# Graph layer with sorted edges: gate, hot logits and own rows move from the bank of the constants to a bank of their own, and the sorting's scratch shrinks to one bank

## Chip, cores, metric

The kernel runs on one core of one Trainium2 chip, as one launch. The metric is the device time of that core in microseconds (us). Engines are called as in the profile: PE (matrix products and transposes; PEld are its weight loads), DVE (vector), ACT (activation), POOL (here it only issues gathers) and SP (issues most DMAs).

## What is computed

A graph layer over 12,500 nodes of 128 features and 412,500 edges that are sorted by destination (`dst`), followed by a residual and a layer norm:

```
theta = x[dst] - x[src]
w     = sigmoid(relu(theta @ W1 + b1) @ W2 + b2)
agg   = segment_sum(w * theta, dst)
indeg = segment_sum(ones, dst)
out   = layernorm(x + agg + indeg * (x @ W4 + b4))
```

## The kernel before

**Stages.** First a table `z` in DRAM is built with, for each node, `x @ W1` beside `x` (`table_chunk`, L748 on). Then the edges are worked through in 276 parts. The first 18 (`PLAIN`) have 1,024 edges each and every source row is gathered for them (`early_part`). Parts 18 to 275 have 1,532 edges each (`part`): 1,024 of these are gathered from `z` by source node, the other 512 have sources in small ranges of nodes, the "hot" ones, and their rows are made from tables in SBUF by products with one-hot tiles. Two parts make one block (104 output rows). `part(s)` is called with `h == 0` for even and `h == 1` for odd `s`; a pair of parts is one round of the main stage.

**One part, engine by engine.** The main loop runs under a manual schedule: PE, DVE and ACT carry out their instructions in the order in which the code issues them, so the order of the lines in `part` is the order of each engine's queue.

- PE: L1076/L1077 (hidden layer of the hot edges of part s+1, into bank `pz`), L885 (`spread_y`: destination rows for the edges of part s+2, into one of two `y` banks), L1090 (`hot_rows`: four hot logits columns of part s+1), L1093 (hot rows turned into `pz`), L1049 (hot products for a later part, into `pd`), then the sums into `pa`: in an even part `add_block` (L1130: `sh`, eight `wxh`, four `wx` products), in an odd part `begin_block` (L1141, L1142, L807, four L1130).
- DVE: L988 (`weigh`: half of the previous part's gathered rows times their gate), L943 (destination minus source rows; this frees the `y` bank that L885 writes next), L948 (relu times `w2_b`), L918 (`one_hot_w`, reads `iota_f`; before L954 in even parts, after it in odd ones), L954 (sum to the logits `lg`); then in an even part L1112 (`one_hot_h`, reads `iota_f`), in an odd part L1195 and at its end `normalize` (L1223 to L1248). Between them stand the steps of the sorting.
- ACT: L1082 (relu of the hot hidden layer, `hr`, which L1090 reads), one-hot tiles L864/L865, in odd parts L1184, L812, L1124, L1125, then L1099 (sigmoid of the hot logits), four L1102 (weighted hot rows), in odd parts L1203/L1205 (`own`: this block's own rows), L960 (`open_gate`: sigmoid of `lg` into `gate`), L966, L970, four L995, then L1033/L1035 (one-hot tiles for L1049), L1063.
- POOL: eight indirect gathers of a part (L398), for part s+3 in `part(s)`. The first of the eight waits for the newest PE instruction at that place (`paced`), the sums of the part before.

**The sorting.** `place` is a generator that splits the edges of the next 64 parts (a set) into hot and gathered ones on DVE, with some PE and ACT. The sets begin at parts 18, 82, 146, 210 and 274; the first is placed during the early parts, the others during the main stage. Each `yield` names a kind of step: "k" for the many short ones (32 rounds of L580, L581, L583 and L576, that work in SBUF alone), "s", "p", "m" and "c" for longer ones. `spend` issues steps at the end of each part against a credit of 2.5 per part, at a price of 0.85 for a "k", 2.5 for an "m" and 3.5 for an "s" or "p". Some steps use a scratch tile in PSUM: the two sums of L534 to L547, the four scans (L636 to L657, an "s" each), the nine moves (L670 to L676, an "m" each) and the transposes L609 and L701. In the main stage the scratch is `px`, a tile of two PSUM banks (1,024 fp32).

**PSUM.** There are eight banks: `fix`, two of `y`, `pz`, `pd`, `pa` and the two of `px`. `fix` holds five things (L290 to L297): `iota_f` and `w2_b`, constants that DVE reads in L918, L1112 and L948; `own_f`, which ACT writes in L1205 and DVE reads and writes in L1223 and reads in L1229; `lgh`, which PE writes in L1090 and ACT reads in L1099; `gate`, which ACT writes in L960 and DVE reads in L988. The language layer that the kernel is written in puts in all semaphores. It orders two accesses from different engines to one PSUM tile also where they touch different columns.

Of the kernel before, what the change touches and what calls it, by code (L numbers as in the profile page):

```python
# [9 lines left out]
F32 = mybir.dt.float32  # L10
BF16 = mybir.dt.bfloat16
F16 = mybir.dt.float16
I32 = mybir.dt.int32
U16 = mybir.dt.uint16
AF = mybir.ActivationFunctionType
OP = mybir.AluOpType
# [4 lines left out]
P = 128  # L21
D = 128
K = 8
# [3 lines left out]
SUB = 2  # L27
WB = 104
# [4 lines left out]
G = 4  # L33
# [16 lines left out]
HX = HB + 1  # L50
RG = 4
HK = HR * HS
HQ = HK // P
# [13 lines left out]
WL = HL + 1  # L67
# [3 lines left out]
HKL = HR * HE  # L71
# [4 lines left out]
MOVES = 9  # L76
# [6 lines left out]
def gnn_resnorm(  # L83
# [37 lines left out]
    nc = tc.nc  # L121
# [3 lines left out]
    NS = PLAIN - (E1 - E) // CE  # L125
# [12 lines left out]
    while n0 < N:  # L138
        t = max(1, (N - n0) // P)
# [115 lines left out]
    w2_c = const.tile([P, 1], F32, name="w2_c")  # L255
# [25 lines left out]
    for i, t in enumerate(terms):  # L281
        at = slice(i * HALF // 2, i * HALF // 2 + 1)
# [7 lines left out]
    cps = ctx.enter_context(tc.tile_pool(name="ps_c", bufs=1, space=bass.MemoryType.PSUM))  # L290
    fix = cps.tile([P, 512], F32, name="fix")
    iota_f = fix[:, :WB].rearrange("p (o m) -> p o m", o=1)
    own_f = fix[:, WB:WB + D]
    w2_b = fix[:, WB + D:WB + 2 * D]
    lgh = fix[:, 512 - 2 * K - SUB * HQ:512 - 2 * K].rearrange("p (i q) -> p i q", q=HQ)
    gate = fix[:, 512 - 2 * K:].rearrange("p (i k) -> p i k", k=K)
    w2_f = w2_r.rearrange("p (o m) -> p o m", o=1)  # L297

    oh_all = const.tile([P, NO * RW], F32, name="oh")
# [57 lines left out]
    for t in wxe_buf:  # L357
        nc.vector.memset(t[:, :, D + 1:], 1.0)
    late_at = 2 * G * P + 2 * K * AW
    assert late_at + 2 * NS <= HX * HK and WB + 2 * D + 2 * K + SUB * HQ <= 512  # L360
    hot_src = const.tile([P, NU, RG * HB * HS], F16, name="hot_src")
    hots = {}

# [7 lines left out]
    def filled(t, s):  # L371

        if s < NF:
            return t
        return t.rearrange("p (h j) d -> p h j d", h=2)[:, :, :JT, :]
# [121 lines left out]
    def place(i, scratch, es, ed, bb, dp):  # L497
# [8 lines left out]
        v = nc.vector  # L506
# [17 lines left out]
        for r in rows:  # L524
            v.scalar_tensor_tensor(b[r, 3:4], c[r, 2:3], float(NOT - WB + 1), c[r, 18:19],
                                   op0=OP.add, op1=OP.add)
        yield "s"

        t = ep.tile([P, WL], F32, name="et")
# [7 lines left out]
        C = -(-HL // 2)  # L537
        for j in range(2):
            at = slice(j * C, min(j * C + C, HL))
            m = at.stop - at.start  # L540
            step = scratch()[:, :m]
            v.tensor_sub(step, ed[:, at.start + 1:at.stop + 1], ed[:, at])
            q = ep.tile([P, P * G], F32, name="eq")[:, :m]
# [30 lines left out]
        for r in range(HR):  # L574
            if r:
                v.scalar_tensor_tensor(left, left, float((HR - r + 1) * AREA), left,  # L576
                                       op0=OP.is_lt, op1=OP.mult)
# [20 lines left out]
                        op0=OP.logical_shift_right, op1=OP.bitwise_and)  # L598
# [12 lines left out]
        for q in range(HQ):  # L611
            for h in range(LISTS):
                a, e = max(h * HKL - q * P, 0), min((h + 1) * HKL - q * P, P)
# [12 lines left out]
        w = ep.tile([P, WL], I32, name="ed")  # L626
        NC = 4
        C = -(-WL // NC)
        assert 3 * C <= WL - HKL // 2 and 2 * HKL <= WL - HKL // 2 and 2 * C < 2 * P * G
        for j in range(NC):  # L630
            at = slice(j * C, min(j * C + C, WL))
            m = at.stop - at.start
            pw = scratch()[:, :2 * P * G]
            odd, count = pw[:, :m + 1], pw[:, C + 1:C + 1 + m]
            keep, out_, mark = (free[:, k * C:k * C + m] for k in range(3))
            v.tensor_scalar(keep, t[:, at], float(NOT * BIG), None, op0=OP.is_ge)  # L636
            v.scalar_tensor_tensor(mark, t[:, at], float(BIG), keep, op0=OP.is_ge, op1=OP.add)
            v.tensor_scalar(mark, mark, -1.0, 1.0, op0=OP.mult, op1=OP.add)
            if j:
                v.tensor_copy(odd[:, :1], c[:, 5:6])  # L640
            else:
                v.memset(odd[:, :1], 0.0)
            v.tensor_tensor_scan(odd[:, 1:], mark, keep, c[:, 5:6] if j else 0.0,
                                 op0=OP.mult, op1=OP.add)
            v.tensor_copy(c[:, 5:6], odd[:, m:])
            v.scalar_tensor_tensor(mark, mark, 0.0, odd[:, :m], op0=OP.is_equal, op1=OP.mult,
                                   accum_out=c[:, 6 + j:7 + j])
            v.tensor_add(keep, keep, mark)
            v.scalar_tensor_tensor(w[:, at], t[:, at], float((2 * NOT - 1) * BIG), keep,
                                   op0=OP.min, op1=OP.mult)  # L650
            v.tensor_scalar(out_, keep, -1.0, 1.0, op0=OP.mult, op1=OP.add)
            v.tensor_tensor_scan(count, out_, most.to_broadcast([P, m]),
                                 c[:, 4:5] if j else 0.0, op0=OP.add, op1=OP.min)
            v.tensor_copy(c[:, 4:5], count[:, m - 1:])
            move = out_.bitcast(I32)
            v.tensor_mul(move, count, keep)
            v.scalar_tensor_tensor(w[:, at], move, 31 - MOVES, w[:, at], op0=OP.logical_shift_left,  # L657
                                   op1=OP.bitwise_or)
            yield "s" if j < NC - 1 else "m"
# [8 lines left out]
        assert SW + HKL < 1 << MOVES and BIG << 8 == 1 << (31 - MOVES) and MOVES % 2 and WL <= 2 * P * G  # L668
        for r, m in enumerate([1 << r for r in range(MOVES)]):
            u = ep.tile([P, WL], I32, name="ew" if r % 2 else "et")  # L670
            bit = scratch().bitcast(I32)[:, :WL]
            v.tensor_scalar(bit, w, MOVES - r, 31, op0=OP.logical_shift_left, op1=OP.arith_shift_right)
            v.scalar_tensor_tensor(u, bit, -1, w, op0=OP.bitwise_xor, op1=OP.bitwise_and)
            v.copy_predicated(u[:, :WL - m].bitcast(F32), bit[:, m:], w[:, m:].bitcast(F32))
            yield "m" if r < MOVES - 1 else "z"
            w = u  # L676
        to = ep.tile([P, WL], I32, name="ed")[:, :BL]
        v.tensor_scalar(to, w[:, :BL], BIG.bit_length() - 1, 2 * NOT - 1,
                        op0=OP.logical_shift_right, op1=OP.bitwise_and)
# [31 lines left out]
    with tc.manual_schedule(engines={SP}), tc.tile_pool(name="work", bufs=2) as wp, tc.tile_pool(  # L711
# [25 lines left out]
        def wide():  # L737

            return ps_l.tile([P, 2 * P * G], F32, name="px")
# [183 lines left out]
        def logits(s):  # L923
# [31 lines left out]
            if s % SUB:  # L955
                one_hot_w(s)

        def open_gate(s):

            nc.scalar.activation(filled(gate[:, s % 2].rearrange("p (k e) -> p k e", e=1), s),  # L960
                                 filled(parts[s]["lg"], s), AF.Sigmoid, bias=b2_c)

        def gate_sums(s):
# [8 lines left out]
        def weigh(s):  # L972

            zs = rows_of(s)
            if s < PLAIN:
                wx = wx_of(s)
                for k in range(K):
                    nc.scalar.activation(wx[:, k, :D], zs[:, k, :] if s < NH else zs[:, k, D:],
                                         AF.Copy, scale=wx[:, k, D:D + 1])
                return  # L980
            w = gate[:, s % 2].rearrange("p (k e) -> p k e", e=1)
            wx = wx_of(s)[:, :, :D]
            if s < NF:
                xs = zs[:, :KV, D:]
                w, wx = w[:, :KV], wx[:, :KV]
            else:
                xs, w, wx = filled(zs[:, :, D:], s), filled(w, s), filled(wx, s)
            nc.vector.tensor_tensor(wx, xs, w.to_broadcast(list(xs.shape)), op=OP.mult)  # L988
# [84 lines left out]
        def hot_turned(t):  # L1073

            xT = xT_all[:, (t - PLAIN) % HX, :]
            nc.tensor.matmul(pz, wneg, xT, start=True, stop=False)  # L1076
            nc.tensor.matmul(pz, y_of(t), blocks[t // SUB]["oh"][:, BP:], start=False, stop=True)  # L1077
# [6 lines left out]
        def hot_rows(t):  # L1084

            xT = xT_all[:, (t - PLAIN) % HX, :]
            hr = parts[t]["hr"]
            for q in range(HQ):
                at = slice(q * P, (q + 1) * P)
                nc.tensor.matmul(lgh[:, t % SUB, q:q + 1], hr[:, at], w2_c, start=True, stop=True)  # L1090
            for q in range(HQ):
                at = slice(q * P, (q + 1) * P)
                newest[0] = nc.tensor.transpose(pz[:, at], xT[:, at], ident)  # L1093

        def hot_weights(t):

            b, h = divmod(t, SUB)
            wx = wxh_buf[b % len(wxh_buf)][:, h * HQ:(h + 1) * HQ, :]
            nc.scalar.activation(wx[:, :, D:D + 1], lgh[:, h].rearrange("p (q e) -> p q e", e=1),  # L1099
                                 AF.Sigmoid, bias=b2_c)  # L1100
            for q in range(HQ):
                nc.scalar.activation(wx[:, q, :D], pz[:, q * P:(q + 1) * P], AF.Copy,  # L1102
                                     scale=wx[:, q, D:D + 1])
# [93 lines left out]
        def own(b):  # L1197

            d = blocks[b]
            a = d["a"]  # L1200
            plain = b * SUB < PLAIN
            sw = wp.tile([P, 2], F32, name="sw")
            nc.scalar.activation(sw[:WB], a[:WB, D:AW], AF.Copy, bias=1.0)  # L1203
            d["own"] = d["xw"][:WB] if plain else own_f[:WB]
            nc.scalar.activation(d["own"], d["xw"][:WB], AF.Copy, scale=sw[:WB, 0:1])  # L1205
            d["deg"] = a[:WB, D + 1:AW] if plain else sw[:WB, 1:]

# [127 lines left out]
        def early_part(s):  # L1335
# [19 lines left out]
            while opened:  # L1355
                hot_out(*opened.pop(0))
            if s == PLAIN - 1:
                hot_turned(PLAIN)
                hot_relu(PLAIN)
            if h and b:  # L1360
# [84 lines left out]
        for t in (wx_buf[EW], *wxh_buf):  # L1445
            nc.vector.memset(t[:, :, D + 1:], 1.0)
        add_up(PLAIN - 1)
        px = wide()
        where[0] = lambda: px

        def spread_ahead(s):

# [273 lines left out]
```

## Time and profile before

| | |
|---|---|
| median of three runs | 3246.63 us (3229.67 to 3252.84) |
| profiled execution: its own time | 3245.33 us |
| profiled execution: span from first to last instruction | 3243.3 us |
| busy in the span | PE 2793.9, DVE 2413.1, ACT 2456.1, POOL 2163.7 us |
| mean granted PE clock | 0.880 |

In a row of a group the columns are line, engine, operation, tiles written and read, count, busy time and mean duration of one, then the engine's idle time before these and what ended it. In a row of the waits they are the engine and line that waited, what it waited for, us in total, times and the longest. A row of the timeline has start and duration in us, engine, line, operation and, in brackets, the idle time before it.

### The profile page before, as it was taken

To read this page: it belongs to the slowest core of one execution; us is meant where nothing else is said; L and a number is where in the kernel's file an instruction comes from. 1 tells how busy PE (TensorE), PEld (TensorE's weight loads), DVE (VectorE), ACT (ScalarE), POOL (GpSimd) and SP (SyncE) were. 2 spreads that over 40 slices of the span, in tenths; PEclk is the share of its full clock that TensorE was granted. 3 is DMA by queue.
4 is the path that set the end of the run, shared out by engine and by line. 5 is a ranking of instruction groups with operands and counts; after the bars stand their busy time and mean duration, and the time that the engine had idled before them with its cause. 6 is when DMAs were issued, how large, how long until landed. Compare 5 with 4: busy or idle time off the path is not lost.

```text
span 3243.3 us, 53854 instructions
## 1 busy us (share of the span) xinstructions
PE 2793.9 (86%) x16422; PEld 2346.8 (72%) x16422; DVE 2413.1 (74%) x4015; ACT 2456.1 (76%) x6397; POOL 2163.7 (67%) x2213
## 2 busy tenths in 40 slices
PE   6868889898888889888898988989898988888896
PEld 5667777777767777777776777767776776777675
DVE  7997677777767877777667787777657778877654
ACT  5447777787788787777887777878887778778875
POOL 3675676776666676766676677766676777766662
PEclk7768888888899898898998889989988899988988
DMA  7564444444444444444454444444444444444441
GB/s 246 159 175 115 116 125 125 118 129 114 126 132 125 120 130 121 123 125 123 131 149 112 124 123 127 129 118 127 122 133 112 126 122 132 129 111 124 127 123 49
DMA packets 239303, 413.24 MB, mean 127 GB/s; under 512 B 63423, under 2 KB 147226, under 8 KB 237470
## 3 DMA queue, kind: packets, MB, share of 16 engines
q0 software_dynamic: 105280, 286.93, 31.8%
q1 hardware_dynamic: 131756, 116.40, 13.9%
q10 hardware_dynamic: 1970, 6.40, 0.6%
q8 instruction: 132, 2.16, 0.3%
q14 instruction: 165, 1.35, 0.1%
HBM read 388.57 MB, written 20.94 MB: 126 GB/s over the span
## 4 chain that ended last, share of the span: by engine, by line


## 5 line engine op out<-in xcount | busy, mean ns | idle before, releaser
L398 POOL DMA_INDIRECT zbuf<-z,src_i x2060 | 2013.1, 977 | 931.3 <-issue 371.9
L1049 PE MATMUL pd<-of,tabs 128*128 128x128 f32 (+2 forms) x4240 | 666.8, 325 | 0.0
L1049 PEld LDWEIGHTS pd<-of,tabs 128*128 128x128 f32 x4240 | 649.7, 242 | 0.0
L1130 PE MATMUL pa<-wx,ow 128*104 128x260 f32 (+1 forms) x2284 | 542.9, 384 | 1.8 <-DVE wx L988 1.8
L1090 PE MATMUL fix<-w_c,hr 128*128 128x1 f32 x2064 | 308.1, 270 | 226.9 <-DVE ow L918 197.7
L885 PEld LDWEIGHTS y<-y,oh 128*128 128x128 f32 (+1 forms) x2108 | 274.7, 196 | 283.4 <-DVE zbuf L943 215.3
L1090 PEld LDWEIGHTS fix<-w_c,hr 128*128 128x128 f32 x2064 | 294.6, 220 | 253.1 <-ACT sh L1125 103.0
L1130 PEld LDWEIGHTS pa<-wx,ow 128*104 128x104 f32 x2284 | 377.7, 180 | 82.9 <-issue 2.9
L1112 DVE TENSOR_TENSOR owh<-fix,hrel 128x832 f32<-128x832 f32 x129 | 132.2, 1025 | 410.5 <-ACT fix L960 398.8
L885 PE MATMUL y<-y,oh 128*128 128x128 f32 (+1 forms) x2108 | 299.1, 286 | 118.6 <-DVE zbuf L943 108.1
L1082 ACT ACTIVATE hr<-pz 128x512 f32<-128x512 f32 x258 | 154.0, 597 | 286.9 <-PE pz L1077 286.8
L1102 ACT ACTIVATE wxh<-pz,wxh 128x128 f32<-128x128 f32 x1032 | 295.2, 369 | 88.7 <-PE pz L1093 86.1
L1033 ACT ACTIVATE of<-hot_src,nodes 128x512 f32<-128x512 f16 (+2 forms) x530 | 343.9, 696 | 3.5 <-PE pd L1049 2.4
L948 DVE SCALAR_TENSOR_TENSOR zbuf<-zbuf,fix 128x1024 f32<-128x1024 f32 x273 | 331.6, 1215 | 13.4 <-ACT wxh L1099 4.1
L954 DVE TENSOR_REDUCE lg<-zbuf 128x8 f32<-128x1024 f32 x273 | 329.9, 1209 | 5.0
L995 ACT ACTIVATE wx<-zbuf,wx 128x128 f32<-128x128 f32 x1028 | 328.7, 390 | 0.0
L943 DVE TENSOR_TENSOR zbuf<-y,zbuf 128x1024 f32<-128x1024 f32 x258 | 313.6, 1216 | 0.0
L1035 ACT ACTIVATE of<-of 128x1024 f32<-128x1024 f32 (+1 forms) x265 | 274.1, 1035 | 8.4
L1076 PE MATMUL pz<-xT,wni 128*128 128x512 f32 x516 | 266.2, 598 | 1.1 <-ACT wxh L1102 1.1
L1077 PE MATMUL pz<-oh,y 128*128 128x512 f32 x516 | 266.3, 598 | 0.2 <-ACT oh L865 0.2
L1130 PE MATMUL pa<-wxh,owh 128*104 128x130 f32 x2064 | 260.0, 280 | 0.0
L1130 PEld LDWEIGHTS pa<-wxh,owh 128*104 128x104 f32 x2064 | 248.0, 175 | 0.0
(302 smaller groups left out, 4103.0 us busy)
## 6 DMA issues: line engine op xcount, KB each, us to landing
to_all<-off_d SPq DMA_DIRECT2D x258, 128.0 KB
zbuf<-z,src_i POOLq DMA_INDIRECT x2060
hot_src<-hot_s SPq DMA_DIRECT2D x228, 128.0 KB
z<-zbuf SPq DMA_DIRECT2D x10, 1024.0 KB
y<-z SPq DMA_DIRECT2D x270, 28.0 KB
xw<-in_x_dram SPq DMA_DIRECT2D x138, 52.0 KB
out_dram<-o SPq DMA_DIRECT2D x138, 52.0 KB
wx<-in_x_dram ACTq DMA_DIRECT2D x12, 512.0 KB
```

What stands on the lines that cost most here:

```text
L398: ins = nc.gpsimd.indirect_dma_start(out=rows_of(s)[:, k, :], out_offset=None, in_=z if s >= NH else x, in_offset=IndirectOffsetOnAxis(ap= ...
L885: nc.tensor.matmul(y[:, j, :], d["oh"][:, (k0 + j) * P:(k0 + j + 1) * P], y_of(s), start=True, stop=True)
L943: nc.vector.tensor_sub(half, yy.to_broadcast([P, 2, n, D]), half)
L948: nc.vector.scalar_tensor_tensor(h[:, at, :], h[:, at, :], 0.0, w2.to_broadcast([P, n, D]), op0=OP.max, op1=OP.mult)
L954: nc.vector.tensor_reduce(lg[:, at, 0], h[:, at, :], AX.X, OP.add)
L995: nc.scalar.activation(wx[:, k, :D], rows_of(s)[:, k, D:], AF.Copy, scale=wx[:, k, D:D + 1])
L1033: nc.scalar.activation(of[:, t, :], hot_src[:, i % NU, :w], AF.Abs, bias=nodes[:, t:t + 1])
L1035: nc.scalar.activation(of, of, AF.Relu, scale=-1.0, bias=1.0)
L1049: newest[0] = nc.tensor.matmul(to[:, q], tabs[:, g * RG + q, t, :], of[:, t, q], start=t == 0, stop=t == HT - 1)
L1090: nc.tensor.matmul(lgh[:, t % SUB, q:q + 1], hr[:, at], w2_c, start=True, stop=True)
L1102: nc.scalar.activation(wx[:, q, :D], pz[:, q * P:(q + 1) * P], AF.Copy, scale=wx[:, q, D:D + 1])
L1130: newest[0] = nc.tensor.matmul(to if len(w.shape) == 3 else to[:, 0, :], one, w, start=first and i == 0, stop=last and i == len(terms) - 1)
```

## The change

`gate`, `lgh` and `own_f` leave `fix`, which keeps the two constants. The tile `px` is allocated earlier (at part 17 in place of the end of the early parts) and split by columns into `halves`, one bank each: the first half is the sorting's scratch in the main stage, the second holds gate, hot logits and own rows. A scratch of 512 columns is too short for the 767 columns of a move, so each move is done in two pieces (512 and 255 columns), six DVE instructions in place of three. The nine moves of the first set, during the early parts, are split as well.

```diff
     fix = cps.tile([P, 512], F32, name="fix")
     iota_f = fix[:, :WB].rearrange("p (o m) -> p o m", o=1)
-    own_f = fix[:, WB:WB + D]
-    w2_b = fix[:, WB + D:WB + 2 * D]
-    lgh = fix[:, 512 - 2 * K - SUB * HQ:512 - 2 * K].rearrange("p (i q) -> p i q", q=HQ)
-    gate = fix[:, 512 - 2 * K:].rearrange("p (i k) -> p i k", k=K)
+    w2_b = fix[:, WB:WB + D]
...
-            pw = scratch()[:, :2 * P * G]
+            pw = scratch()
...
-            bit = scratch().bitcast(I32)[:, :WL]
-            v.tensor_scalar(bit, w, MOVES - r, 31, op0=OP.logical_shift_left, op1=OP.arith_shift_right)
-            v.scalar_tensor_tensor(u, bit, -1, w, op0=OP.bitwise_xor, op1=OP.bitwise_and)
-            v.copy_predicated(u[:, :WL - m].bitcast(F32), bit[:, m:], w[:, m:].bitcast(F32))
+            for a in range(0, WL, P * G):
+                e = min(a + P * G, WL)
+                bit = scratch().bitcast(I32)[:, :e - a]
+                v.tensor_scalar(bit, w[:, a:e], MOVES - r, 31, op0=OP.logical_shift_left, op1=OP.arith_shift_right)
+                v.scalar_tensor_tensor(u[:, a:e], bit, -1, w[:, a:e], op0=OP.bitwise_xor, op1=OP.bitwise_and)
+                f = max(a, m)
+                v.copy_predicated(u[:, f - m:e - m].bitcast(F32), bit[:, f - a:], w[:, f:e].bitcast(F32))
...
+        halves = []
+
+        def gate():
+
+            return halves[1][:, :2 * K].rearrange("p (i k) -> p i k", k=K)
+
+        def lgh():
+
+            return halves[1][:, 2 * K:2 * K + SUB * HQ].rearrange("p (i q) -> p i q", q=HQ)
+
...
-            d["own"] = d["xw"][:WB] if plain else own_f[:WB]
+            d["own"] = d["xw"][:WB] if plain else halves[1][:WB, P * G - D:]
...
             if s == PLAIN - 1:
+                px = wide()
+                halves.extend(px[:, i * P * G:(i + 1) * P * G] for i in range(2))
                 hot_turned(PLAIN)
                 hot_relu(PLAIN)
...
         add_up(PLAIN - 1)
-        px = wide()
-        where[0] = lambda: px
+        where[0] = lambda: halves[0]
```

The other lines of the diff call `gate()` and `lgh()` where `gate` and `lgh` stood (L960, L988, L1090, L1099).

More of the change, by code (lines that the diff above doesn't have):

```diff
@@ L359, in gnn_resnorm @@
     late_at = 2 * G * P + 2 * K * AW
-    assert late_at + 2 * NS <= HX * HK and WB + 2 * D + 2 * K + SUB * HQ <= 512
+    assert late_at + 2 * NS <= HX * HK and WB + D <= 512
     hot_src = const.tile([P, NU, RG * HB * HS], F16, name="hot_src")
@@ L628, in place @@
         C = -(-WL // NC)
-        assert 3 * C <= WL - HKL // 2 and 2 * HKL <= WL - HKL // 2 and 2 * C < 2 * P * G
+        assert 3 * C <= WL - HKL // 2 and 2 * HKL <= WL - HKL // 2 and 2 * C < P * G
         for j in range(NC):
@@ L956, in logits @@
                 one_hot_w(s)
+        halves = []
[3 more added lines that the diff above has]
+            return halves[1][:, 2 * K:2 * K + SUB * HQ].rearrange("p (i q) -> p i q", q=HQ)
         def open_gate(s):
-            nc.scalar.activation(filled(gate[:, s % 2].rearrange("p (k e) -> p k e", e=1), s),
+            nc.scalar.activation(filled(gate()[:, s % 2].rearrange("p (k e) -> p k e", e=1), s),
                                  filled(parts[s]["lg"], s), AF.Sigmoid, bias=b2_c)
@@ L980, in weigh @@
                 return
-            w = gate[:, s % 2].rearrange("p (k e) -> p k e", e=1)
+            w = gate()[:, s % 2].rearrange("p (k e) -> p k e", e=1)
             wx = wx_of(s)[:, :, :D]
@@ L1089, in hot_rows @@
                 at = slice(q * P, (q + 1) * P)
-                nc.tensor.matmul(lgh[:, t % SUB, q:q + 1], hr[:, at], w2_c, start=True, stop=True)
+                nc.tensor.matmul(lgh()[:, t % SUB, q:q + 1], hr[:, at], w2_c, start=True, stop=True)
             for q in range(HQ):
@@ L1098, in hot_weights @@
             wx = wxh_buf[b % len(wxh_buf)][:, h * HQ:(h + 1) * HQ, :]
-            nc.scalar.activation(wx[:, :, D:D + 1], lgh[:, h].rearrange("p (q e) -> p q e", e=1),
+            nc.scalar.activation(wx[:, :, D:D + 1], lgh()[:, h].rearrange("p (q e) -> p q e", e=1),
                                  AF.Sigmoid, bias=b2_c)
```

## The prediction

> **What bounds the kernel now.** I read the page first (busy shares, the clock line), then the waits, then one pair of parts in the timeline, then the windows of the same pair.
>
> ```profile
> span 3243.3 us, 53854 instructions
> DVE  7997677777767877777667787777657778877654
> PEclk7768888888899898898998889989988899988988
> ```
>
> No engine is full: PE is busy for 2793.9 of 3243.3 us, DVE mostly for 7 tenths. So the cause must be the engines' waits for each other.
>
> ```profile
> DVE owh L1112 <- ACT fix L960: 398.8, 126, 7.8
> POOL zbuf L398 <- PE pa L1130: 311.7, 118, 11.6
> PEld y L885 <- DVE zbuf L943: 215.3, 133, 10.9
> DVE fix L1223 <- ACT fix L960: 211.2, 115, 4.9
> PE fix L1090 <- DVE ow L918: 197.7, 121, 7.4
> ACT wxh L1099 <- PE fix L1090: 196.1, 102, 5.5
> PE y L885 <- DVE zbuf L943: 108.1, 60, 10.1
> ```
>
> Three of these carry no data. L1090 writes hot logits and L918 reads a constant; L1112 reads the same constant and L960 writes the gate: they wait because all lie in `fix`. Now one pair during a "k" stretch of the sorting, odd part first:
>
> ```profile
> 1301.25 1.22 DVE L943 TENSOR_TENSOR zbuf<-y,zbuf 128x1024 f32<-128x1024 f32 x1
> ...
> 1302.45 0.60 ACT L1082 ACTIVATE hr<-pz 128x512 f32<-128x512 f32 x1 [1.50 <-PE pz L1077]
> ...
> 1302.52 0.97 PEld L885 LDWEIGHTS y<-y,oh 128*128 128x128 f32 x8 [0.93 <-DVE zbuf L943]
> ...
> 1305.14 0.29 ACT L1125 ACTIVATE sh<-sh 104x104 f32<-104x104 f32 x1
> ...
> 1305.59 0.95 DVE L580 MAX8 ed<-ew 128x8 f32<-128x767 f32 x1
> ...
> 1305.62 1.58 PE L1090 MATMUL fix<-w_c,hr 128*128 128x1 f32 x8 [1.94 <-DVE ow L918]
> ...
> 1307.94 3.62 PE L1049 MATMUL pd<-of,tabs 128*128 128x128 f32 x16
> 1308.25 1.14 ACT L1102 ACTIVATE wxh<-pz,wxh 128x128 f32<-128x128 f32 x4 [0.75 <-PE pz L1093]
> ...
> 1309.92 0.27 ACT L960 ACTIVATE fix<-lg,b_c 128x8 f32<-128x8 f32 x1
> ...
> 1310.22 0.30 DVE L1223 TENSOR_TENSOR fix<-fix,a 104x128 f32<-104x128 f32 x1 [1.43 <-ACT fix L960]
> ...
> 1311.60 0.68 DVE L988 TENSOR_TENSOR wx<-zbuf,fix 128x512 f32<-128x512 f32 x1
> ...
> 1312.20 1.22 DVE L943 TENSOR_TENSOR zbuf<-y,zbuf 128x1024 f32<-128x1024 f32 x1
> ...
> 1314.19 1.02 PE L1076 MATMUL pz<-xT,wni 128*128 128x512 f32 x2
> ...
> 1315.09 1.21 DVE L954 TENSOR_REDUCE lg<-zbuf 128x8 f32<-128x1024 f32 x1
> ...
> 1315.90 1.05 PE L885 MATMUL y<-y,oh 128*128 128x128 f32 x8
> ...
> 1316.79 1.01 PE L1090 MATMUL fix<-w_c,hr 128*128 128x1 f32 x8
> ...
> 1318.14 1.95 PE L1049 MATMUL pd<-of,tabs 128*128 128x128 f32 x16
> ...
> 1319.41 0.29 ACT L960 ACTIVATE fix<-lg,b_c 128x8 f32<-128x8 f32 x1
> ...
> 1319.73 1.02 DVE L1112 TENSOR_TENSOR owh<-fix,hrel 128x832 f32<-128x832 f32 x1 [3.44 <-ACT fix L960]
> ...
> 1320.67 0.95 DVE L580 MAX8 ed<-ew 128x8 f32<-128x767 f32 x1
> ...
> 1321.93 1.92 PE L1130 MATMUL pa<-wx,ow 128*104 128x260 f32 x8
> ...
> 1323.68 0.59 PE L1076 MATMUL pz<-xT,wni 128*128 128x512 f32 x1
> 1323.79 0.68 DVE L988 TENSOR_TENSOR wx<-zbuf,fix 128x512 f32<-128x512 f32 x1
> ```
>
> In the odd part PE waits 0.93 us at L885 and 1.94 us at L1090; behind that the same 16 matmuls of L1049 take 3.62 us, against 1.95 us in the even part. The windows of the two parts show why:
>
> ```profile
> 1301.25:1312.20 10.95, 8.91 (x44) 7.77 (x43) 9.24 (x18) 7.06 (x22) 8.43 (x9) 0.71 0.41 112
> 1312.20:1324.40 12.20, 12.20 (x77) 10.06 (x77) 8.62 (x13) 9.99 (x23) 7.64 (x8) 0.98 0.49 130
> ```
>
> (PE, PEld, DVE, ACT, POOL busy, then the granted clock.) After the two gaps the clock is 0.71 on average, in the even part 0.98. So the wait at L1090 costs twice: its own time and about 3 us of slow matmuls. The even part is long because PE, full all the time, is behind, and because DVE does nothing for 3.44 us before L1112 and has L1112 and the sorting still to do between L960 and L988.
>
> The Trainium skill (TensorE: Matmul & The Clock Gate, Part 1) has the clock halved only after about an idle window of 3.4 us, and warns of gaps over 3 us. By that rule gaps of 0.93 and 1.94 us would leave the clock alone, and the change would return at most the idle 197.7 us of L1090: 3048 us. The rows differ: the 3.62 us stand behind these gaps.
>
> **The change, part by part.** What the built program of the changed kernel waits for matters more than the diff. L1090 no longer waits for L918, but for L1082 alone; L1112 waits for nothing on other engines; L1099 waits for L988 of its part, long done, in place of L918. L1223 still waits for L960 (both in the new bank), and L988 needs its gate anyway. And there is a new wait: `px` is one tile, and the program orders its two halves against each other. Each sorting step that uses the scratch now waits for L960 of its own part (36 moves, 16 scans and a few more), and the transposes L609 and L701 wait for it on PE, in 8 places, at the end of PE's list where L960 is done.
>
> *A pair without scratch steps*, reckoned from the rows; zero is the end of L943, all at full clock. PE's spacings are those of the even part: L885 to L1090 0.89, to L1049 1.35, to L1076 5.54, to the next L885 1.71 (1314.19 to 1315.90): 9.5 us from L885 to L885. Of this the sums take 3.6 (1320.09 to 1323.68); the odd part has four `wx` products in their place, 1.92, and an estimated 0.4 for L1141 to L807: 8.2 us.
> - Odd: L1090 starts at 0.94, not 3.15; `hr` (L1082) is there at 0.58. ACT finishes L1125 at 2.96, then 0.27 for L1099 and 1.94 from the start of L1102 to the end of L960: 5.2, before 7.7. DVE starts L580 at 3.1, needs 3.1 for it and the two steps behind it (1320.67 to 1323.79), and is at L1223 at 6.3, no longer waiting. With 1.38 from L1223 to L988 and 1.82 from there to the end of L943, the next L943 ends at 9.5, before 10.95.
> - Even: L960 ended 2.9 us after L1090 started, so at 3.85, before 6.3. DVE goes from L954 (2.9) straight into L1112 (3.8) and the sorting (6.9), and ends L943 at 8.8, before 12.2.
>
> DVE's list in the pair is then 18.3 us, PE's 17.7 us, both under POOL's. What is late next is POOL:
>
> ```profile
> 1303.12 0.95 POOL L398 DMA_INDIRECT zbuf<-z,src_i  x1 [0.30 <-DMA zbuf<-z,src_i]
> 1304.37 0.95 POOL L398 DMA_INDIRECT zbuf<-z,src_i  x1 [0.30 <-issue]
> ```
>
> ```profile
> L1112 DVE TENSOR_TENSOR owh<-fix,hrel x129: 1024/1025/1027, 313.0 to 3218.6; 128x832 f32<-128x832 f32 x129
> ```
>
> (A count, then shortest, median and longest in ns, then the first and the last start.) Gathers follow each other at 1.25 us, 16 in a pair: 20.0 us. The pair now takes (3218.6 - 313.0) / 128 = 22.70 us; that POOL waits 311.7 us for PE's sums says the same: this is all that can be won before the gathers set the pace. ACT is at 17.05 us in the pair shown and its odd list is longer than PE's, so that L1082 comes late by a microsecond now and then. I take 20.4 us (the floor and 0.4 for this and for a residue of slow clock). The bounds are 20.0, and 21.7: at POOL's pace of 10.0 us for a part PE waits 1.8 us for the even part's L943, and if that halves the clock as in the pair shown, L1090 and L1049 lose 0.57 and 1.67, 2.2 us, and PE's 17.7 + 1.8 + 2.2 set the pace.
>
> *A pair with scratch steps.* 13 steps (9 moves, 4 scans) and a few more in each of four sets: some 60 parts, 30 pairs. The odd part loses: before, such a step ran while L960 was awaited; now it runs after. A move is longer, too:
>
> ```profile
> L673 DVE SCALAR_TENSOR_TENSOR ew<-px,et 128x767 int32<-128x767 int32 x20 | 19.1, 957 | 0.7
> L637 DVE SCALAR_TENSOR_TENSOR ew<-et,ew 128x192 f32<-128x192 f32 (+1 forms) x20 | 7.3, 364 | 0.7
> ```
>
> Between these two rows lie 1.03 ns for a column, so that 512 columns take 0.69 and 255 columns 0.43 us: 1.12 in place of 0.96, 3.4 us for a move of three in place of 2.9. Odd: from L960 at 5.2, 3.4 for the move, 1.38, 1.82: L943 ends at 11.8. PE, ready after 8.2, waits 3.6 us at L885. Even: PE's 9.5 to the next L885, 0.6 behind L943. The pair is 21.3 us at full clock; but 3.6 us is a longer gap than those shown, so that I count one slow stretch of 2.2 us, which delays the next L960 and all behind it: 23.5 us. The bounds are 21.3 and, with two such stretches, 25.7.
>
> *The early parts.* The first set's nine moves become 9 x 0.5 = 4.5 us longer on a DVE that is at 9 tenths there (slices 2 and 3): I count all of it; at least nothing. The earlier allocation of `px` costs nothing, since nothing else uses it after the first set has been placed.
>
> *The sum.* 99 pairs at 22.7 - 20.4 = 2.3: -228. 30 pairs at 23.5 - 22.7 = 0.8: +24. Early: +4.5. Together -200, from the profiled execution's own 3245.3 us (span 3243.3): **3045 us**. The median of the runs, 3246.6, is 1.3 us above it, which is ignored.
>
> The Trainium skill (PSUM — Partial Sum Buffer, PSUM bank collisions raise a hardware error) asks for an order between engines by bank and quadrant, not by tile; the two halves of `px` would then need none, and the scratch pairs would fall to 20.4 us too, some 2953 us. The built program has those waits, so this has no chance of its own.
>
> **Rivals.**
> - *The wait moves to L885.* PE gets to L885 sooner and waits there for L943: these waits are 323 us already. For it: in the reckoning DVE is 1.3 us behind PE in each odd part. Against it: L943 itself comes 1.5 to 3.4 us sooner. If each pair keeps a slow stretch, 99 pairs at 21.7 save 99, less 24 and 4.5: 3175 us.
> - *It doesn't do what it says: no change.* L988 takes over L1112's wait for L960, and L1090 waits for `hr` of a late ACT. For it: ACT waited 196.1 us for L1090 only, and has work for three quarters of the time. Against it: in the odd part L1082 ended at 1303.05, 2.6 us before L1090 started. About 3245 us.
> - *Slower: the scratch waits.* DVE stands at a move until L960, PE behind it at L885, the clock at half. If scratch pairs cost 25.7 us (+90) and the others win nothing, with 4.5 early: 3340 us. It decides only if the other 99 pairs win less than 0.95 us each; the reckoning gives them 2.3.
>
> **How the numbers follow.** The forecast (2930 to 3110) has 0.62, the moved wait (to 3213) 0.18, no change 0.09, the scratch waits 0.11. A measurement of this kernel tells about 1% (32 us) from no change. Faster by over 1%: 0.80; within: 0.09; slower: 0.11. The low end is POOL's floor, 3245.3 - 311.7 = 2934; the high end lies in the moved wait, where 99 pairs at 21.85 save 84 and the rest costs 28.5: 3190. The range is 2930 to 3190.
>
> **What would show it.** In the changed profile the rows L1090 <- L918 and L1112 <- L960 are gone; the granted clock of the main stage is above 0.9; POOL's wait for L1130 is under 100 us; the moves and scans wait for L960 in some tens of places. Wrong would be: L885 <- L943 far above 323 us (the wait moved), a clock at 0.88 or below, or L988 <- L960 near 400 us.

## The result and the profile after

The changed kernel takes **3165.47 us** (median of four runs, 3158.64 to 3170.73), the kernel before beside it 3249.74 us (3229.67 to 3256.18): a ratio of **0.975**, 95% interval 0.970 to 0.980. It is 2.5% faster, not 6.2%: 120 us of the forecast gain of 200 did not come. The profiled execution took 3168.71 us, with a span of 3166.6 us.

In the changed kernel's file the lines behind L960 have moved by ten: L960 is now L970, L988 L998, L1049 L1059, L1076/L1077 L1086/L1087, L1082 L1092, L1090 L1100, L1112 L1122, L1130 L1140, L1223 L1233. L885, L918, L943, L948 and L954 are the same, and the gathers' L398 is L395. A move begins at L671, the scans' scratch steps at L637.

From the page of the changed kernel, the span and the slices of DVE and of the clock:

```profile
span 3166.6 us, 53729 instructions
DVE  7998689887757988877557898877567888877555
PEclk7868899988888999988888999988898999988898
```

The slices now alternate: stretches at 0.9 with a busy DVE, and stretches at 0.8. Before, both rows were more even. A selection of its waits (engine and line that waited, what for, us in total, times, the longest; the rows of PEld and PE at L885 cover largely the same waits):

```profile
PEld y L885 <- DVE zbuf L943: 359.5, 135, 11.6
PE y L885 <- DVE zbuf L943: 246.4, 128, 10.8
POOL zbuf L395 <- PE pa L1140: 223.0, 46, 13.1
DVE px L1233 <- ACT px L970: 120.2, 81, 3.8
DVE px L671 <- ACT px L970: 92.4, 33, 3.8
DVE wx L998 <- ACT px L970: 60.1, 39, 7.2
PE px L1100 <- ACT hr L1092: 58.9, 78, 2.4
DVE wx L998 <- ACT rel L705: 37.7, 4, 11.3
DVE px L1233 <- PE px L701: 35.4, 4, 9.2
DVE px L637 <- ACT px L970: 25.3, 11, 2.9
```

The two waits that the change was to remove are gone: L1100 waits for `hr` alone, and L1122, the largest row before (398.8 us), has no row any more. Two things stand in their place. The wait at L885 has grown from 215.3 and 108.1 us to 359.5 and 246.4. And there are waits that the kernel before did not have at all: the moves (L671) and the scans (L637) wait for the gate (L970), and, the other way round, the own rows (L1233) and L998 wait for the sorting's transposes (L701, L705). All of these are between the two halves of `px`.

**Pair by pair.** The main stage is a sequence of pairs of parts. I cut the trace at the starts of L1112 (L1122 after), where DVE makes an even part's hot one-hot tiles, 128 pairs, and sorted them by which of the sorting's lines begin in them. This grouping is mine, from the trace's records; mean us of a pair:

| kind of pair | pairs | before | forecast | after |
|---|---|---|---|---|
| sorting without scratch ("k" steps) | 67 | 22.48 | 20.4 | 19.96 |
| no sorting | 16 | 20.92 | 20.4 | 20.70 |
| scratch: scans | 12 | 22.67 | 23.5 | 24.12 |
| scratch: moves | 16 | 22.61 | 23.5 | 25.19 |
| scratch: last move and transposes L701 | 4 | 25.78 | 23.5 | 30.77 |
| scratch: sums, other transposes | 13 | 25.20 | 20.4 | 26.74 |

The "k" pairs do what was forecast, and a little better. Half of them take under 18.9 us, less than the 20.0 of 16 gathers: by the trace only 14 or 15 gathers start in such a pair, and 18 or 19 in nine of the eleven longer pairs of 23 to 24 us between them. The pairs draw on parts that POOL has gathered ahead, and it catches up later. One such pair after, even part first (start, duration, engine, line):

```profile
1305.63 1.22 DVE L943 TENSOR_TENSOR zbuf<-y,zbuf 128x1024 f32<-128x1024 f32 x1
...
1308.56 1.05 PE L1100 MATMUL px<-w_c,hr 128*128 128x1 f32 x8 [0.50 <-ACT hr L1092]
...
1309.65 1.01 DVE L1122 TENSOR_TENSOR owh<-fix,hrel 128x832 f32<-128x832 f32 x1
...
1309.95 1.95 PE L1059 MATMUL pd<-of,tabs 128*128 128x128 f32 x16
...
1314.29 1.22 DVE L943 TENSOR_TENSOR zbuf<-y,zbuf 128x1024 f32<-128x1024 f32 x1
...
1319.44 1.95 PE L1059 MATMUL pd<-of,tabs 128*128 128x128 f32 x16
...
1324.52 1.22 DVE L943 TENSOR_TENSOR zbuf<-y,zbuf 128x1024 f32<-128x1024 f32 x1
```

From L943 to L943 the even part takes 8.66 us (forecast 8.8, before 12.20), the odd part 10.23 (forecast 9.5, before 10.95), and the 16 matmuls of L1059 take 1.95 us in both. Now an odd part with a move, and the start of the even part behind it:

```profile
835.33 1.22 DVE L943 TENSOR_TENSOR zbuf<-y,zbuf 128x1024 f32<-128x1024 f32 x1
...
838.86 1.05 PE L885 MATMUL y<-y,oh 128*128 128x128 f32 x8
...
843.89 0.27 ACT L970 ACTIVATE px<-lg,b_c 128x8 f32<-128x8 f32 x1
844.19 0.69 DVE L671 TENSOR_SCALAR px<-et 128x512 int32<-128x512 int32 x1 [3.79 <-ACT px L970]
...
849.18 0.68 DVE L998 TENSOR_TENSOR wx<-zbuf,px 128x512 f32<-128x512 f32 x1
849.78 1.22 DVE L943 TENSOR_TENSOR zbuf<-y,zbuf 128x1024 f32<-128x1024 f32 x1
...
851.05 2.08 PE L885 MATMUL y<-y,oh 128*128 128x128 f32 x8 [4.14 <-DVE zbuf L943]
...
852.92 1.71 PE L1100 MATMUL px<-w_c,hr 128*128 128x1 f32 x8
```

DVE has the move ready to go and stands still for 3.79 us, until ACT has written the gate into the other half of `px`. Behind the move come L998 and L943, and PE waits 4.14 us for L943. Then the clock is at half: L885 takes 2.08 us instead of 1.05, L1100 1.71 instead of 1.01. Over the 45 scratch pairs the time at half clock goes from 5.3 to 8.4 us a pair; over the "k" pairs it falls from 4.7 to 1.6.

### The profile page after: what moved, and what is told of

Its sections match the earlier page's. It is cut to its first block, busy times and chain, and to the rows that moved or that the text cites. A ratio compares the mean times of both kernels' runs of the same rounds, so it can differ in the third digit from the quotient of the medians.

```text
span 3166.6 us, 53729 instructions
## 1 busy us (share of the span) xinstructions
PE 2736.3 (86%) x16422; PEld 2294.6 (72%) x16422; DVE 2435.9 (77%) x4150; ACT 2441.9 (77%) x6397; POOL 2157.0 (68%) x2213
## 4 chain that ended last, share of the span: by engine, by line
## 5 line engine op out<-in xcount | busy, mean ns | idle before, releaser
L395 POOL DMA_INDIRECT zbuf<-z,src_i x2060 | 2007.3, 974 | 868.5 <-issue 385.4
L1059 PE MATMUL pd<-of,tabs 128*128 128x128 f32 (+2 forms) x4240 | 620.9, 310 | 0.0
L885 PEld LDWEIGHTS y<-y,oh 128*128 128x128 f32 (+1 forms) x2108 | 297.6, 212 | 426.1 <-DVE zbuf L943 359.5
L1059 PEld LDWEIGHTS pd<-of,tabs 128*128 128x128 f32 x4240 | 601.6, 227 | 0.0
L885 PE MATMUL y<-y,oh 128*128 128x128 f32 (+1 forms) x2108 | 328.8, 305 | 253.5 <-DVE zbuf L943 246.4
L1140 PE MATMUL pa<-wx,ow 128*104 128x260 f32 (+1 forms) x2284 | 534.9, 380 | 1.8 <-DVE wx L998 1.8
L1140 PEld LDWEIGHTS pa<-wx,ow 128*104 128x104 f32 x2284 | 369.6, 176 | 80.5 <-issue 2.9
L1092 ACT ACTIVATE hr<-pz 128x512 f32<-128x512 f32 x258 | 153.8, 596 | 314.7 <-PE pz L1087 314.6
L1100 PE MATMUL px<-w_c,hr 128*128 128x1 f32 x2064 | 302.5, 268 | 63.5 <-ACT hr L1092 58.9
L1100 PEld LDWEIGHTS px<-w_c,hr 128*128 128x128 f32 x2064 | 295.3, 220 | 79.5 <-ACT hr L1092 74.0
L1043 ACT ACTIVATE of<-hot_src,nodes 128x512 f32<-128x512 f16 (+2 forms) x530 | 344.4, 697 | 7.0 <-PE pd L1059 3.1
L948 DVE SCALAR_TENSOR_TENSOR zbuf<-zbuf,fix 128x1024 f32<-128x1024 f32 x273 | 331.6, 1215 | 9.3
L1112 ACT ACTIVATE wxh<-pz,wxh 128x128 f32<-128x128 f32 x1032 | 294.4, 368 | 53.0 <-PE pz L1103 48.4
L954 DVE TENSOR_REDUCE lg<-zbuf 128x8 f32<-128x1024 f32 x273 | 329.7, 1208 | 5.0
L943 DVE TENSOR_TENSOR zbuf<-y,zbuf 128x1024 f32<-128x1024 f32 x258 | 313.5, 1215 | 12.3 <-DMA zbuf<-z,src_i 12.2
L998 DVE TENSOR_TENSOR wx<-zbuf,px 128x512 f32<-128x512 f32 x258 | 175.9, 682 | 122.2 <-ACT px L970 60.1
L1086 PE MATMUL pz<-xT,wni 128*128 128x512 f32 x516 | 266.7, 599 | 1.1 <-ACT wxh L1112 1.1
L1087 PE MATMUL pz<-oh,y 128*128 128x512 f32 x516 | 267.2, 600 | 0.2 <-ACT oh L865 0.2
L1140 PE MATMUL pa<-wxh,owh 128*104 128x130 f32 x2064 | 262.2, 281 | 0.0
L1140 PEld LDWEIGHTS pa<-wxh,owh 128*104 128x104 f32 x2064 | 252.2, 178 | 0.0
```

Source lines behind the costliest of these rows:

```text
L395: ins = nc.gpsimd.indirect_dma_start(out=rows_of(s)[:, k, :], out_offset=None, in_=z if s >= NH else x, in_offset=IndirectOffsetOnAxis(ap= ...
L885: nc.tensor.matmul(y[:, j, :], d["oh"][:, (k0 + j) * P:(k0 + j + 1) * P], y_of(s), start=True, stop=True)
L943: nc.vector.tensor_sub(half, yy.to_broadcast([P, 2, n, D]), half)
L948: nc.vector.scalar_tensor_tensor(h[:, at, :], h[:, at, :], 0.0, w2.to_broadcast([P, n, D]), op0=OP.max, op1=OP.mult)
L954: nc.vector.tensor_reduce(lg[:, at, 0], h[:, at, :], AX.X, OP.add)
L1043: nc.scalar.activation(of[:, t, :], hot_src[:, i % NU, :w], AF.Abs, bias=nodes[:, t:t + 1])
```

## The experiments

Theory W: the loss lies in the wait between the two halves of `px`, which are two banks but one tile. Rival S: it lies in the moves themselves, which are longer in two pieces. All ratios are to the kernel before, run beside them on the same chip.

**Two tiles.** The changed kernel, with one tile for each bank:

```diff
-        def wide():
+        def wide(i=0):
...
-            return ps_l.tile([P, 2 * P * G], F32, name="px")
+            return ps_l.tile([P, P * G], F32, name=("px", "pv")[i])
...
-                px = wide()
-                halves.extend(px[:, i * P * G:(i + 1) * P * G] for i in range(2))
+                halves.extend(wide(i) for i in range(2))
```

(The table stage's transposes, which filled both banks at once, take the two tiles in turn.)

> The changed kernel with the two halves of px as two tiles of one bank each (the table's transposes use one of the two for every four columns), so that a scratch step of the sorting has no wait for the gate (L960 of before). Theory W, the wait between the two halves makes the 45 pairs of parts with scratch steps slow (25.85 us against 23.66 before the change): these pairs come down to 20 to 21.5 us, the other pairs stay at about 20, total 2940 to 2990 us. Rival S, the moves in two pieces are what makes them slow: nothing changes in the main stage, 3140 to 3170 us.

Measured: **2997.93 us**, ratio 0.924 (0.921 to 0.928), 167 us less than the changed kernel (on another chip; by the ratios, 0.924 against 0.975, it is 5.1% of the kernel before). Its moves no longer wait:

```profile
L671 DVE TENSOR_SCALAR px<-et 128x512 int32<-128x512 int32 (+1 forms) x40 | 22.5, 563 | 0.8
L637 DVE COPY px<-col 128x1 f32<-128x1 f32 x15 | 2.3, 151 | 0.0
```

against, in the changed kernel (the last column is the idle time ahead of the instructions, and what ended it):

```profile
L671 DVE TENSOR_SCALAR px<-et 128x512 int32<-128x512 int32 (+1 forms) x40 | 22.4, 561 | 57.3 <-ACT px L970 56.5
L637 DVE COPY px<-col 128x1 f32<-128x1 f32 x15 | 2.4, 160 | 25.3 <-ACT px L970 25.3
```

The instructions are the same, in number and duration; only the waits are gone. Pairs with moves fall from 25.19 to 19.43 us, with scans from 24.12 to 20.10, all scratch pairs from 25.85 to 21.47. Theory W holds, though the time lies 8 us above its range, and S falls: the moves are still split. What is left at POOL:

```profile
POOL zbuf L395 <- PE pa L1140: 56.5, 25, 11.0
```

With 56.5 us of waits for PE, and 20.85 us for the mean pair against the 20.0 of 16 gathers, the gathers themselves are now close to being the bound.

**The split alone.** The kernel before, with only the moves in two pieces (the third hunk of the diff).

> The kernel before with the moves in two pieces and nothing else. Theory W: the six instructions in place of three add 0.5 us for a move, 36 moves in the main stage and 9 early, partly hidden in DVE's waits for the gate: 3250 to 3280 us. Rival S: the 45 pairs with scratch steps go from 23.7 to about 25.9 us, 3340 us.

Measured: 3254.73 us, ratio 1.0044 (1.0023 to 1.0066). This is where theory W had it, and far from S's 3340 us. By the ratio the split costs 14 us by itself; the pairs with moves go from 22.61 to 23.80 us, while each other kind moves by less than 0.6 us, most of them down.

**One half of the move at a time,** both on the two-tile kernel. First with the hot logits alone moved out of `fix` (gate and own rows stay):

```diff
+    own_f = fix[:, WB:WB + D]
+    w2_b = fix[:, WB + D:WB + 2 * D]
+    gate_f = fix[:, 512 - 2 * K:].rearrange("p (i k) -> p i k", k=K)
...
-            return halves[1][:, :2 * K].rearrange("p (i k) -> p i k", k=K)
+            return gate_f
...
-            d["own"] = d["xw"][:WB] if plain else halves[1][:WB, P * G - D:]
+            d["own"] = d["xw"][:WB] if plain else own_f[:WB]
```

> Two tiles, but only the hot logits leave the bank of the constants; gate and own rows stay in fix. So PE's L1090 is free of VectorE's one-hots, while L1112 still waits for the gate and scratch steps for nothing new. If PE's gap at the logits and the slow clock behind it are the main loss, most of the gain comes here: 3000 to 3080 us. If VectorE's wait before L1112 is the main loss: 3180 to 3250 us.

Measured: 3044.65 us, ratio 0.940 (0.936 to 0.943). Then with gate and own rows alone moved out (the logits stay):

```diff
+    lgh_f = fix[:, 512 - SUB * HQ:].rearrange("p (i q) -> p i q", q=HQ)
...
-            return halves[1][:, 2 * K:2 * K + SUB * HQ].rearrange("p (i q) -> p i q", q=HQ)
+            return lgh_f
```

> Two tiles, but only gate and own rows leave the bank of the constants; the hot logits stay in fix. L1112 no longer waits for the gate, L1090 still waits for L918. If VectorE's wait before L1112 is the main loss: 3000 to 3080 us. If PE's gap at the logits is: 3150 to 3250 us. If only both together count, this one and the logits-only one are both over 3150 us.

Measured: 3047.26 us, ratio 0.940 (0.936 to 0.944). The rows of the waits that stay, first with the logits moved, then with gate and own rows moved (the lines here lie one or two further on: L1124 and L1123 make the hot one-hot tiles, L1101 the hot logits):

```profile
DVE owh L1124 <- ACT fix L972: 296.2, 124, 8.1
POOL zbuf L397 <- PE pa L1142: 124.0, 45, 11.0
```

```profile
DVE owh L1123 <- ACT wxh L1110: 157.9, 122, 5.8
PE fix L1101 <- DVE ow L919: 127.7, 144, 7.5
POOL zbuf L396 <- PE pa L1141: 125.2, 51, 11.1
```

Each half alone brings 6.0%, both together 7.6%: neither dominates, against what I had expected. The pairs tell why the two do not add up. By the same grouping the 83 pairs without scratch steps take 20.41 us in both runs, and 20.50 with both halves moved: either half alone is enough to bring them near the gathers' 20.0, although in the first run DVE still idles 296.2 us at the one-hot tiles. The rest of the difference lies in the scratch pairs, 22.52 and 22.65 us here against 21.47 with both.

**A gap filled.** Is the price of a scratch pair its chain of waits, or the slow clock behind the gap? In the changed kernel, PE repeats the hidden layer of the hot edges (the same products into `pz`, with the same result) three more times before L885, in an even part behind a scratch step; by the trace one repeat takes 1.7 us of PE. `used` is set when a scratch step is issued:

```diff
             if t < NS:
                 hot_turned(t)
+                if used and h == 0:
+                    for _ in range(3):
+                        hot_turned(t)
+            used.clear()
```

This kernel and two with another batch size (taken up below) were first run on a chip on which the kernel before itself took 3759.86 us.

> The changed kernel, with PE kept busy in the gap behind a scratch step: where the odd part before has issued a step that uses the scratch, an even part carries out L1086 and L1087 (the hidden layer of the hot edges) four times in place of once, with the same result; 3 x 1.02 us of matmuls at full clock lie in the gap of about 4 us in which L885 waits for L943. Question: are the 25.85 us of a pair with scratch steps (23.66 before) the price of the slow clock behind the gap, or of the chain L970, scratch step, L998, L943, L885 itself? Theory C (the clock): half-clock time in these 45 pairs falls from 8.4 us to 4 or less, the pair to about 23.5 us, 45 x 2.3 = 105 us in all, so about 3060 us. Theory D (the chain): half-clock time falls as well, but the pair stays between 25 and 26.5 us, and the time within 1% of 3165 us.

> The kernel with two scratch tiles (2997.9 us), with the layer norm's square roots taken for ten blocks at once in place of five (LB 10), so that ACT loads its tables for Sqrt and back for Sigmoid half as often (1.28 us each, two in five pairs; such a pair took about 23.6 us, its neighbours 19 to 20.5). Theory T (the table loads are on the path): some 13 pairs fall from 23.6 to 20.5 us, 40 us in all, about 2958 us. Theory G (the gathers at 1.25 us set the pace, and a pair that is late is caught up out of the parts gathered ahead): no more than 10 us, 2988 to 2998 us.

> The changed kernel (3165.5 us) with square roots for ten blocks at once in place of five. Here pairs without scratch steps run at 18.9 us, those with table loads at 23 to 24 us. Theory T: some 13 pairs fall by about 4 us (those with scratch steps among them by less), 40 to 52 us in all, about 3115 to 3125 us. Theory G (behind the gathers, which at 20.0 us a pair are slower than 18.9 in any case, a late pair is caught up): within 10 us of 3165.

Measured there: 3858.49 us, ratio 1.026 (1.024 to 1.028); 3710.67 us, 0.987 (0.984 to 0.989); 3806.35 us, 1.013 (1.009 to 1.017). Nothing of the question can be read from these. The "k" pairs take 25.4 to 25.5 us in all three, and each has a wait that no kernel has elsewhere, the first of these two rows of the filled one (`remote`: the profile knows nothing that ended it):

```profile
ACT of L1043 <- remote: 488.3, 172, 4.5
POOL zbuf L395 <- PE pa L1140: 698.6, 136, 19.2
```

L1043 reads `hot_src`, which DMAs fill. What makes this chip slow was not settled. The three were run again elsewhere, with the changed kernel beside them:

> The changed kernel once more, beside the three that follow, on whatever chip they get: in the runs e5_filled_gap, e6_two_tiles_lb10 and e7_after_lb10 the kernel before itself took 3760 us (3238 to 3250 elsewhere), and the changed kernel had no run beside them. Expected on a chip like the first ones: ratio 0.975 to before, 3160 us. On a chip like that of e5 to e7, where pairs without scratch steps take 25.4 us in every kernel: about 1.01.

Measured: 3169.69 us, ratio 0.976 (0.971 to 0.981); the kernel before took 3240.98 us. The result repeats.

> The kernel of e5_filled_gap again (PE repeats L1086/L1087 three times in the gap behind an odd part's scratch step). Theory C (slow clock is the price of the scratch pairs): about 105 us under r0_after. Theory D (the chain from L970 over the scratch step to L885): within 1% of r0_after, with less half-clock time.

Measured: 3142.20 us, ratio 0.969 (0.964 to 0.974): 27 us less than the changed kernel beside it, with 444 more matmuls. In total that is theory D's case, a change of 0.9% and less half-clock time (from 8.7 to 2.8 us per scratch pair), but the kinds of pairs differ. Pairs with moves go from 25.19 to 22.84 us, with scans from 24.22 to 22.10: there theory C holds (28 pairs, 63 us). But pairs with the last move and the transposes go from 30.76 to 33.40, and those with the first transposes (L606, L609 before) from 26.02 to 29.45. There L1092 has to wait for the added products, and ACT's copies of the transposes (L705, L612) stand behind L1092 in its list. DVE's L998 waits for them, again because they share `px`, for 33.2 and 26.5 us, where the changed kernel beside it has 11.8 and 9.2:

```profile
DVE wx L998 <- ACT src_i L705: 33.2, 4, 8.6
DVE wx L998 <- ACT hrel L612: 26.5, 4, 6.7
```

(These pair times come from one execution of each; the two lie 48 us apart, where the medians lie 27 apart.) The odd part with a move and the even part behind it, in this kernel:

```profile
837.39 0.27 ACT L970 ACTIVATE px<-lg,b_c 128x8 f32<-128x8 f32 x1
837.69 0.69 DVE L671 TENSOR_SCALAR px<-et 128x512 int32<-128x512 int32 x1 [2.50 <-ACT px L970]
...
845.40 1.05 PE L885 MATMUL y<-y,oh 128*128 128x128 f32 x8
...
846.29 1.01 PE L1100 MATMUL px<-w_c,hr 128*128 128x1 f32 x8
```

The move still waits for L970, but 2.50 us instead of 3.79, and L885 and L1100 run at full clock. So part of the 3.79 was itself the slow clock's, as I read these rows: PE, late from the slow part before, makes `hr` late, ACT writes the gate late, and the move begins late, which makes the next gap.

**Fewer table loads.** Every five pairs ACT loads a table for a square root and another one back, and a pair without scratch steps behind such a square root mostly takes 23 to 24 us where its neighbours take 19. In the changed kernel:

```profile
1326.37 1.28 ACT L1250 ACT_TABLE_LOAD   x1
1328.39 0.60 ACT L1092 ACTIVATE hr<-pz 128x512 f32<-128x512 f32 x1
1329.04 1.87 PE L1100 MATMUL px<-w_c,hr 128*128 128x1 f32 x8 [2.10 <-ACT hr L1092]
1330.37 1.28 ACT L1109 ACT_TABLE_LOAD   x1
...
1331.66 3.62 PE L1059 MATMUL pd<-of,tabs 128*128 128x128 f32 x16
```

The edit is `LB = 10` in place of `LB = 5` (the layer norm's square roots for ten blocks at once), on the two-tile kernel and on the changed one:

> The kernel of e6_two_tiles_lb10 again (two scratch tiles, square roots for ten blocks at once). Theory T (table loads are on the path): ratio to before 0.924 - 0.012 = 0.912. Theory G (late pairs are caught up, the gathers set the pace): 0.921 to 0.925.

Measured: 3005.06 us, ratio 0.926 (0.922 to 0.931), against 0.924 (0.921 to 0.928) with five.

> The kernel of e7_after_lb10 again (the changed kernel, square roots for ten blocks at once). Theory T: 40 to 52 us under r0_after, ratio to before about 0.96. Theory G: within 10 us of r0_after.

Measured: 3174.92 us, ratio 0.979 (0.974 to 0.983), against 3169.69 us beside it. The loads fall by half (L1250 from 29 to 15), and the "k" pairs stay at 19.97 us on average (20.00 with five). Theory G holds, within a few us of its ranges: with fewer long pairs the others are longer (the median "k" pair takes 20.1 us instead of 18.9), since 16 gathers, a pair's mean share, take 20.0 us. A pair of 24 us, in which POOL does 18 or 19 gathers, is time that the pairs of 18.9 us with 14 or 15 had borrowed. The two-tile kernel is the fastest that was found; between five and ten blocks the intervals of the ratios decide nothing.

## Why the forecast was wrong, step by step

- *L1090 no longer waits for L918, nor L1112 for L960.* Right; both rows are gone.
- *A pair without scratch steps falls to 20.4 us.* Right where the sorting runs its "k" steps: 19.96, 67 pairs. The reckoned parts, 9.5 and 8.8 us, came out at 10.23 and 8.66 in the pair shown. Nor did the clock halve there.
- *"99 pairs at 22.7 - 20.4 = 2.3".* **This term failed.** 22.70 us is the mean over all pairs, and the 83 without scratch steps were at 22.18. The 16 pairs without sorting already took 20.92 before (as I read it, because DVE had nothing else to do after L1112 and the wait cost little); they won 0.2. Of the 13 pairs with sums and transposes I had counted nearly all among the 99 ("and a few more"); they took 25.20 before and take 26.74. Only the 67 "k" pairs won 2.5 us.
- *"30 pairs at 23.5".* **This term failed by its size.** The count was good for moves and scans (32), and that they lose was right, but they take 25.49 us on average (12 x 24.12, 16 x 25.19, 4 x 30.77), not 23.5. The move itself came out as reckoned: the mean piece of L671 takes 0.56 us. My upper bound was 25.7, with two slow stretches instead of one. I had let the move begin 5.2 us behind L943; in the odd part shown the gate is there after 844.16 - 836.55 = 7.6 us, since PE starts L885 late (838.86, where I had it at the end of L943). With the gap filled, and so at full clock, the same distance is 837.66 - 831.99 = 5.7 us. One slow stretch thus seems to make the next one; I had it end after 2.2 us.
- By the table the miss is, forecast to measured: "k" pairs 67 x 0.44 = 29 us better, no sorting 16 x 0.3 = 5 worse, moves and scans 32 x 1.99 = 64 worse, the other 13 pairs 13 x 6.34 = 82 worse: 122 us in all, for the 120 between 3045 and 3165. Counted from before to after, the 83 pairs without scratch steps gave 172 us and the 45 with them cost 99, where the forecast had 228 and 24.
- *The transposes cost nothing.* Wrong. I had asked what they wait for, and not what waits for them: with the gate and the own rows in the same tile, L1233 and L998 wait for L701 and its reader L705, 35.4 + 37.7 us in eight places. The 8 pairs with L701 lost 5.0 and 6.1 us each. With two tiles these waits are gone, yet the pairs behind the last move, in which L701 alone begins, still take 24.84 us there (20.24 before). By the trace 19 to 21 gathers start in each of them, against 13 to 16 before, and at 1.25 us apart these alone fill 24 to 26 us; what else holds the pairs was not tried.
- *The early parts lose 4.5 us.* Not to be told from one execution each: L1112 first starts at 313.0 us before and at 316.8 with the split alone, which would fit, but L1122 at 310.5 after and at 311.5 when the changed kernel was run again. What made up for the longer moves is open.
- *POOL sets the floor.* Right as a floor: POOL still waits 223.0 us for PE after, 56.5 with two tiles, and fewer long pairs (table loads) no longer help.
- *Signs named ahead.* The main stage's clock is above 0.9, if barely (0.91, next row; 0.89 before); POOL's wait is above 100 us; L885's is far above 323 us (605.9 by the same sum of two rows); the moves and scans wait for the gate in 44 places. A large L885 was to mean that the wait had moved there, and the rival of that name forecast 3175 us, near the result. But its mechanism, a slow stretch in every pair, is not what happened: of PE's wait at L885 the scratch pairs hold 194 us after (77 before), the 67 "k" pairs 42 (19 before), by the same grouping.

```profile
300.00:3150.00 2850.00, 2520.34 (x15249) 2106.72 (x15248) 2172.69 (x3566) 2287.91 (x6037) 1991.20 (x2043) 0.91 0.47 127
```

- *The rule beside the sum.* The Trainium skill (PSUM — Partial Sum Buffer, PSUM bank collisions raise a hardware error) asks for an order by bank and quadrant, so that the two halves of `px` need none. I had worked out 2953 us for that, and gave it no chance, since the built program has the waits. Two tiles, with no order between the two banks, give 2998: this agrees with the rule, and it was the tile, not the bank, that held the halves together.

## What to carry to other kernels

A tile is the unit by which the language layer orders engines: two banks in one tile wait for each other as if they were one, and splitting the tile was worth twice the whole change (5.1% beside 2.5%). Before a saving is multiplied by a count, sort the rounds by what runs in them: a mean over all rounds hides those that cannot win, and a wait that is moved must be asked in both directions, for what waits and for what is waited for. A gap on PE can be paid more than once, when its slow clock delays the very step that caused it; but work put into the gap must not stand ahead of something that others wait for.

## What the runs showed of the hardware

- **The clock drops on gaps shorter than its window.** The clock records of the trace show only full and half clock, in stretches of whole multiples of 3.413 us. A stretch of 6.83 us at half begins 0.24 us before the 4.14 us gap shown above ends, and another 0.36 us before the 2.10 us wait behind the table load ends; behind that wait L1059 takes 3.62 us in place of 1.95. I laid the main stage of the kernel before on a grid of 3.413 us. In the 109 windows that were followed by a drop, PE was busy for 0.43 of the time (median); 89 of them lie at 0.44 or below, the others reach up to 0.89. Of the 567 that were followed by full clock none lies below 0.43, and 95 in 100 lie above 0.67. The two overlap, so the busy share alone does not give the exact rule. A return to full clock followed a window with PE busy through all of it (109 of 109). The Trainium skill (TensorE: Matmul & The Clock Gate, Part 1: The HAM clock gate) states the free-running window of 3413 ns, with which this agrees, and a drop after an idle window; here windows that were busy for four tenths were enough.
- **The total of a wait is not its price.** The one-hot tiles idled 398.8 us before. With 296.2 us of that left and PE's hot logits freed, 6.0% of the 7.6% were won; with the one-hot tiles no longer waiting for the gate, and the hot logits still waiting 127.7 us, it was 6.0% too.
- **Chips differ.** On one the kernel before took 3760 us instead of 3238 to 3250, with ACT waiting 488 to 623 us in the three kernels profiled there at L1043, which reads a tile that DMAs fill; elsewhere the profiles have no such wait. The cause is open.
